# A graph kernel whose neighbour aggregation is reorganised: nodes ordered by degree, smaller sorting networks, neighbour lists from packed words

## The chip, the core and the metric

The kernel runs on one core of a Trainium2 chip. A core has a matrix engine (TensorE, in the profile PE, with its weight loads listed apart as PEld), a vector engine (VectorE, DVE), an engine for functions of one input (ScalarE, ACT), GpSimd (POOL), which here issues the gathers, and SyncE (SP), which issues the plain transfers. Each engine works through its own instructions in order; semaphores tie the engines together. The metric is device time in microseconds (us), lower is better.

## What is computed

The input is 16 graphs (B) of 1,024 nodes (N) with 64 channels (C): `x` is 16 x 1024 x 64, `adj` is 16 x 1024 x 1024 of zeros and ones, symmetric, ones on the diagonal, and every node is unmasked. An edge between two different nodes is drawn with probability 0.0078125 on each side of the diagonal and then mirrored, from a fixed seed. Two layers follow each other, each closed by a layer norm over the channels of "input plus layer output".

```python
# layer 0, cut to what matters
nb = (adj > 0) & ~eye                       # neighbours without the node itself
m = nb.sum(-1); rank = cumsum(nb) - 1
skip = where(m > 10, (m + 1) // 2, 1)
removed = nb & (skip > 1) & mask & ((rank + 1) % skip == 0)
adj_d = where(removed | removed.T, 0, adj_with_self_loops)
sv = sort(where(adj_d > 0, x[neighbour], big))          # per node and channel
agg = 0.25*q(0.25) + 0.5*q(0.5) + 0.25*q(0.75)          # interpolated quantiles of sv
x = layernorm(x + (relu((x + agg) @ W1 + b1) @ W2 + b2) * mask)
# layer 1
x = layernorm(x + (tanh(concat(x, adj @ x) @ V1 + c1) @ V2 + c2))
```

So each node drops at most two of its neighbours (and loses those that dropped it), and then, channel by channel, takes a weighted sum of three quantiles of what its remaining neighbours and itself hold.

## The kernel before, in words

Nodes lie along the 128 partitions, eight tiles (NT) of 128 nodes per graph. The 16 graphs are unrolled. A scheduler places each engine's instructions; buffers in rotating pools decide how far one graph's work may run into the next.

**Which neighbours stay.** `dilate` (L125-164) loads one row tile of `adj` after another, transposes it on TensorE into `adj_t` for layer 1, and finds on VectorE, with a prefix sum (L143) and two comparisons (L156, L157), what each row removes. `neighbours` (L166-176) transposes the removals on TensorE, combines them with what the row keeps (L173) and counts the row (`deg`).

**The list of neighbours.** For each row tile, L317 multiplies the 0/1 row by "1024 minus column", and five rounds of MAX8 (L319) and MATCH_REPLACE8 (L321) over all 1,024 columns pull out up to K = 40 neighbour numbers, the node itself among them. Empty places get a number that no row of `x` has.

**Gather, sort, weigh.** `terms(t)` (L328-339) fills a tile `g` of 40 slots x 64 channels with a large number (L330), issues 40 indirect transfers from GpSimd (L332), each of which fetches one slot's row of `x` for the 128 nodes and skips the empty ones, and sorts the 40 slots with a bitonic network on VectorE (`sort40`, L258-284; `exchange`, L243-256; L255 is the minimum and L256 the maximum of a pair). L338 multiplies the sorted slots by the quantile weights. There are three buffers for `g`.

**The rest of both layers.** `finish` (L190-240) sums the 40 weighted slots with 40 f32 matmuls against the identity (L199), runs the two small dense layers (L202, L206), a layer norm (L178-188), the message matmul against `adj_t` (L225), the second small network (L229, L233) and the second layer norm.

**The general path.** `degree` holds every node's count. At the end its maximum is read into a register (L345-352), and `tc.If(largest > K)` (L354) guards a second implementation that recomputes all nodes of all graphs without a limit on neighbours. It is a loop over the 16 graphs, and within it a loop over the 64 channels (L373). One turn of the inner loop:

- VectorE copies the channel (`x_c`), TensorE transposes it into a row along every partition with 8 matmuls, ScalarE copies that out in two halves (`x_r`);
- for each of 8 node tiles k, VectorE writes whether node k comes no later than node j, for all j: comparisons over the tiles before k and after k (L387, L389) and two instructions of 128 x 128 on the diagonal (L390, L392);
- for each of 8 row tiles and 2 halves of 512 nodes (16 units), TensorE counts with 8 bf16 matmuls of 128 x 512 how many valid neighbours come no later (`p_cnt`, two buffers); ScalarE makes of that, for each of the three quantiles, an absolute value with a bias per partition (L407) and a rectified 1 - |.| (L408), into `u` (two buffers); VectorE adds the three up with their shares, multiplies by the 0/1 row, and multiplies by `x_r` with a running sum;
- VectorE adds the two halves into `agg`.

After the 64 channels `finish` runs for that graph. In the program this code stands once; the loops repeat it.

Of the kernel before, what the change touches and what calls it, by code (L numbers as in the profile page):

```python
# [1 line left out]

# [7 lines left out]
F32 = mybir.dt.float32  # L10
F16 = mybir.dt.float16
BF16 = mybir.dt.bfloat16
# [7 lines left out]
P = 128  # L20
K = 40          # neighbours that the sorted path holds per node
BIG = 8.0e37    # sorts behind every value of a node feature; its weight is 0
OOB = 65536.0   # an index that no row of x has: the gather skips it
# [3 lines left out]
EPS = 1e-5  # L27


@with_exitstack  # L30
def kernel(
# [24 lines left out]
    rows = ctx.enter_context(tc.tile_pool(name="rows", bufs=2))  # L56
    held = ctx.enter_context(tc.tile_pool(name="held", bufs=NT))
    work = ctx.enter_context(tc.tile_pool(name="work", bufs=2))
    ps_t = ctx.enter_context(tc.tile_pool(name="ps_t", bufs=2, space=PSUM))
    ps_m = ctx.enter_context(tc.tile_pool(name="ps_m", bufs=2, space=PSUM))  # L60

# [7 lines left out]
    upper = const.tile([P, P], F32, name="upper")  # row <= column  # L69
# [3 lines left out]
    ones_row = const.tile([P, N], BF16, name="ones_row")  # L73
    nc.vector.memset(ones_row, 1.0)
    down = const.tile([P, N], F32, name="down")  # N - column
    nc.gpsimd.iota(down, pattern=[[-1, N]], base=N, channel_multiplier=0,
                   allow_small_or_imprecise_dtypes=True)
    slot = const.tile([P, K], F32, name="slot")
    nc.gpsimd.iota(slot, pattern=[[1, K]], base=0, channel_multiplier=0,
                   allow_small_or_imprecise_dtypes=True)  # L80
    big = const.tile([P, 1], F32, name="big")
    nc.vector.memset(big, BIG)
    eps = const.tile([P, 1], F32, name="eps")
    nc.vector.memset(eps, EPS)
    degree = const.tile([P, B * NT], F32, name="degree")
# [21 lines left out]
    # node mask: a node per partition, a tile of nodes per column  # L107
# [5 lines left out]
    mask_p = ps_m.tile([P, 512], F32, name="mask_p", tag="m")  # L113
    nc.tensor.transpose(mask_p[:, :B * NT], mask_f, ident[:B * NT, :B * NT])
    nc.scalar.copy(mask, mask_p[:, :B * NT])
# [4 lines left out]
    def load_x(b):  # L120
        t = work.tile([P, NT, C], F32, name="x_s")
        nc.sync.dma_start(t, x[b].rearrange("(t p) c -> p t c", p=P))
        return t

    def dilate(adj_b, mask_b):  # L125
        """The neighbours that stay by each row's own rule, those it removes, and adj transposed."""
        adj_t = work.tile([P, NT, N], F32, name="adj_t", bufs=1)
        kept, removed = [], []
        for t in range(NT):
# [12 lines left out]
            rank = rows.tile([P, N], F16, name="rank", bufs=1)  # from 1; exact up to 2048  # L142
            nc.vector.tensor_tensor_scan(rank, ones_row, nb, 0.0, op0=ALU.mult, op1=ALU.add)  # L143
            # skip = ceil(m / 2); ranks skip and 2 * skip go where m > T_THRESH and the mask is set
# [21 lines left out]
    def neighbours(t, kept, removed, deg):  # L166
        """Row tile t of the dilated adjacency, self-loops included, as 0 and 1; its row sums."""
        blk = slice(t * P, (t + 1) * P)
        p = ps_t.tile([P, N], BF16, name="p_rem", tag="tr")
        for j in range(NT):  # L170
            nc.tensor.transpose(p[:, j * P:(j + 1) * P], removed[j][:, blk], ident_h)  # L171
        v = rows.tile([P, N], BF16, name="valid")
        nc.vector.scalar_tensor_tensor(v, p, 0.5, kept[t], op0=ALU.is_lt, op1=ALU.mult, accum_out=deg)  # L173
        nc.vector.tensor_add(v[:, blk], v[:, blk], ident_h)
        nc.vector.tensor_scalar(deg, deg, 1.0, None, op0=ALU.add)
        return v

    def layer_norm(s, dst):  # L178
        st = work.tile([P, 3, NT], F32, name="ln_st")
        nc.vector.tensor_reduce(st[:, 0], s, AX.X, ALU.add)  # L180
        nc.vector.tensor_scalar(st[:, 0], st[:, 0], 1.0 / C, None, op0=ALU.mult)
        nc.vector.tensor_sub(s, s, bcast(st[:, 0], C))
        sq = work.tile([P, NT, C], F32, name="ln_sq", bufs=1)
        nc.scalar.activation(sq, s, AF.Square)
        nc.vector.tensor_reduce(st[:, 1], sq, AX.X, ALU.add)
        nc.scalar.activation(st[:, 2], st[:, 1], AF.Sqrt, bias=eps, scale=1.0 / C)
        nc.vector.reciprocal(st[:, 2], st[:, 2])
        nc.vector.tensor_mul(dst, s, bcast(st[:, 2], C))

    def finish(out_b, x_s, mask_b, adj_t, terms):  # L190
        """Both layers from the aggregates on: terms(t) are the matrices whose sum is tile t's."""
        p_y = ps_m.tile([P, NT, C], F32, name="p_y", tag="y", bufs=1)
        for h in range(2):
            g_t = work.tile([C, HALF], F32, name="g_t")
            for t in range(HT):
                p = ps_m.tile([P, 512], F32, name="p_g", tag="g", bufs=1)
                todo = terms(h * HT + t)
                for i, term in enumerate(todo):
                    nc.tensor.matmul(p[:C, :P], term, ident, start=(i == 0), stop=(i == len(todo) - 1))  # L199
                nc.scalar.copy(g_t[:, t * P:(t + 1) * P], p[:C, :P])  # L200
            p = ps_m.tile([P, 512], F32, name="p_h", tag="m")
            nc.tensor.matmul(p[:H, :HALF], w1a_s, g_t, start=True, stop=True)  # L202
            h_t = work.tile([H, HALF], F32, name="h_t")
            nc.scalar.activation(h_t, p[:H, :HALF], AF.Relu, bias=b1a_c)
            for t in range(HT):
                nc.tensor.matmul(p_y[:, h * HT + t, :], h_t[:, t * P:(t + 1) * P], w2a_s,  # L206
                                 start=True, stop=True)
        y = work.tile([P, NT, C], F32, name="y", bufs=1)
        nc.vector.tensor_add(y, p_y, b2a_r[:, None, :].to_broadcast([P, NT, C]))
        nc.vector.tensor_mul(y, y, bcast(mask_b, C))  # L210
        nc.vector.tensor_add(y, y, x_s)
        x1 = work.tile([P, NT, C], F32, name="x1", bufs=1)
        layer_norm(y, x1)

        p_d = ps_m.tile([P, NT, C], F32, name="p_d", tag="y", bufs=1)
        for h in range(2):
            cols = slice(h * HALF, (h + 1) * HALF)
            node_t = work.tile([2 * C, HALF], F32, name="node_t")
            p = ps_m.tile([P, 512], F32, name="p_x", tag="m")
            for t in range(HT):  # L220
                nc.tensor.transpose(p[:C, t * P:(t + 1) * P], x1[:, h * HT + t, :], ident)
            nc.scalar.copy(node_t[:C], p[:C, :HALF])
            p = ps_m.tile([P, 512], F32, name="p_msg", tag="m")
            for j in range(NT):
                nc.tensor.matmul(p[C:2 * C, :HALF], x1[:, j, :], adj_t[:, j, cols],  # L225
                                 start=(j == 0), stop=(j == NT - 1))
            nc.scalar.copy(node_t[C:], p[C:2 * C, :HALF])
            p = ps_m.tile([P, 512], F32, name="p_z", tag="m")
            nc.tensor.matmul(p[:C, :HALF], w1b_s, node_t, start=True, stop=True)  # L229
            z_t = work.tile([C, HALF], F32, name="z_t")  # L230
            nc.scalar.activation(z_t, p[:C, :HALF], AF.Tanh, bias=b1b_c)
            for t in range(HT):
                nc.tensor.matmul(p_d[:, h * HT + t, :], z_t[:, t * P:(t + 1) * P], w2b_s,  # L233
                                 start=True, stop=True)
        d = work.tile([P, NT, C], F32, name="d", bufs=1)
        nc.vector.tensor_add(d, p_d, b2b_r[:, None, :].to_broadcast([P, NT, C]))  # L236
        nc.vector.tensor_add(d, d, x1)
        o = work.tile([P, NT, C], F32, name="o")
        layer_norm(d, o)
        nc.sync.dma_start(out_b.rearrange("(t p) c -> p t c", p=P), o)  # L240

# [1 line left out]
    def exchange(dst, src, lo, n, k, j, up):  # L243
        """Compare-exchange over slots lo .. lo + n at distance j; blocks of k slots go upward
        and downward in turn, or all the way that `up` says."""
        s = src[:, lo:lo + n, :].rearrange("p (q k) c -> p q k c", k=k)
        d = dst[:, lo:lo + n, :].rearrange("p (q k) c -> p q k c", k=k)
        ways = ((0, 2, True), (1, 2, False)) if up is None else ((0, 1, up),)
        for first, step, asc in ways:
            if first >= n // k:  # L250
                continue
            sv = s[:, first::step].rearrange("p q (m two j) c -> p q m two (j c)", two=2, j=j)
# [194 lines left out]
```

## Time and profile before

| | |
|---|---|
| time, median of 3 runs | 12,840.29 us (12,827.75 to 12,854.84) |
| span of the profiled execution | 11,693.4 us |
| mean granted TensorE clock | 0.580 of full speed |
| VectorE | 9,848.3 us busy, 84% of the span |
| GpSimd | 6,903.3 us busy, 59% |
| TensorE | 2,196.3 us busy, 19% |
| ScalarE | 664.9 us busy, 6% |
| indirect gathers (L332) | 5,120, mean 1,348 ns |
| general path (L354-418) | no instruction of it in the trace |

The profiled execution's span runs from its first to its last instruction; no separate time is given for that execution, and the median of the timed runs lies 1,146.9 us above its span. Busy shares are averages over stages; the span is cut below by stage. A group's line reads: program line, engine, operation, output <- input, shapes, count, then busy time and mean of one, then the idle time of that engine just before and what ended it.

### The profile page before, as it was taken

Reading aid. Unit: us, or ns where it says so; the run is one execution under the profiler, and the core shown is the slowest. Engines: PE = TensorE matmul, PEld = TensorE weight load, DVE = VectorE, ACT = ScalarE, POOL = GpSimd, SP = SyncE. Lnnn points to the kernel's source line nnn. Section 1 sums busy time; section 2 is a strip of 40 time slices with the busy share of each in tenths; the row PEclk is TensorE's granted clock in tenths of the full one; section 3 lists DMA queues with packets and bytes.
Section 4 is the critical chain, followed back from the end, with each engine's and each line's share of the span. In section 5 each row is a group of like instructions: output and inputs, shape, how many; then the busy total and the mean of one; then the engine's idle time right before and its main releaser. Section 6 shows DMA issues by size and latency. Waiting matters only on the chain. (4 is left out here: it accounts for less than half of the span.)

```text
span 11693.4 us, 53638 instructions
## 1 busy us (share of the span) xinstructions
PE 2196.3 (19%) x13826; PEld 1809.5 (15%) x13826; DVE 9848.3 (84%) x12969; ACT 664.9 (6%) x835; POOL 6903.3 (59%) x5130
## 2 busy tenths in 40 slices
PE   1121111211112121121211212112121221211212
PEld 1111111111111111111111112111120111101111
DVE  8888888888888888888888888888888888888887
ACT  0000000000000000000000000000000000000000
POOL 5828558285582855828558284582846828468284
PEclk5565555655556555565555655556565555655556
DMA  1000000000000000000000000000000000000000
GB/s 30 7 19 7 5 22 7 19 7 5 22 7 19 7 4 22 7 18 7 5 22 7 18 8 5 22 7 19 8 5 22 7 20 7 5 22 7 12 7 5
DMA packets 216974, 141.12 MB, mean 12 GB/s; under 512 B 164598, under 2 KB 180495, under 8 KB 216656
## 3 DMA queue, kind: packets, MB, share of 16 engines
q0 software_dynamic: 163840, 61.91, 2.9%
q1 hardware_dynamic: 52816, 75.71, 2.1%
q8 instruction: 110, 1.80, 0.1%
q14 instruction: 208, 1.70, 0.0%
HBM read 239.27 MB, written 4.19 MB: 21 GB/s over the span
## 5 line engine op out<-in xcount | busy, mean ns | idle before, releaser
L332 POOL DMA_INDIRECT g<-in_x_dram,idx x5120 | 6901.2, 1348 | 4648.6 <-issue 4546.5
L255 DVE TENSOR_TENSOR h<-g 128x512 f32<-128x512 f32 (+4 forms) x1920 | 1754.2, 930 | 1359.3 <-DMA g<-in_x_dram,idx 1358.9
L199 PE MATMUL p_g<-ident,h 128*64 128x128 f32 x10240 | 1430.9, 312 | 7457.8 <-DVE h L338 7457.8
L199 PEld LDWEIGHTS p_g<-ident,h 128*64 128x64 f32 x10240 | 1400.0, 162 | 7487.9 <-DVE h L338 7487.9
L255 DVE TENSOR_TENSOR g<-h 128x512 f32<-128x512 f32 (+4 forms) x1920 | 1813.7, 947 | 0.2
L256 DVE TENSOR_TENSOR g<-h 128x512 f32<-128x512 f32 (+4 forms) x1920 | 1813.8, 947 | 0.0
L256 DVE TENSOR_TENSOR h<-g 128x512 f32<-128x512 f32 (+4 forms) x1920 | 1753.5, 930 | 0.0
L319 DVE MAX8 key<-code 128x8 f32<-128x1024 f32 x640 | 753.4, 1211 | 0.0
L330 ACT COPY g<-big 128x2560 f32<-128x2560 f32 x128 | 297.3, 2324 | 6679.3 <-DVE h L338 6679.3
L321 DVE MATCH_REPLACE8 code<-key,code 128x1024 f32<-128x1024 f32 x512 | 616.4, 1208 | 0.0
L171 PE MATMUL p_rem<-ident_h,removed 128*128 128x128 bf16 x1024 | 142.9, 299 | 1752.4 <-DVE removed L159 903.8
L171 PEld LDWEIGHTS <-removed 128*128 128x128 bf16 x1024 | 98.7, 134 | 1795.6 <-DVE removed L159 927.4
L338 DVE TENSOR_TENSOR h<-g,qw 128x2560 f32<-128x2560 f32 x128 | 360.2, 2814 | 0.0
L236 DVE TENSOR_TENSOR d<-p_d,b2b_r 128x512 f32<-128x512 f32 x16 | 11.1, 692 | 367.9 <-PE p_d L233 367.9
L143 DVE TENSOR_TENSOR_SCAN rank<-ones_row,nb 128x1024 f16<-128x1024 bf16 x128 | 292.3, 2283 | 0.5
L225 PE MATMUL p_msg<-adj_t,x 128*64 128x512 f32 x512 | 255.4, 657 | 0.0
L137 PE MATMUL p_adj<-ident,a 128*128 128x128 f32 x1024 | 156.8, 298 | 78.1 <-DMA a<-in_adj_dram 63.2
L296 ACT ACTIVATE hat<-hat 128x320 f32<-128x320 f32 x48 | 22.5, 470 | 2542.2 <-DVE hat L295 2542.2
L157 DVE SCALAR_TENSOR_TENSOR hit<-rank,s,hit 128x1024 bf16<-128x1024 f16 x128 | 164.1, 1282 | 3.5
L317 DVE TENSOR_TENSOR code<-valid,down 128x1024 f32<-128x1024 bf16 x128 | 154.8, 1212 | 0.0
L173 DVE SCALAR_TENSOR_TENSOR valid<-p_rem,kept 128x1024 bf16<-128x1024 bf16 x128 | 154.2, 1214 | 0.0
L138 ACT COPY adj_t<-p_adj 128x512 f32<-128x512 f32 x256 | 140.5, 586 | 70.7 <-PE p_adj L137 69.8
(88 smaller groups left out, 1797.1 us busy)
## 6 DMA issues: line engine op xcount, KB each, us to landing
g<-in_x_dram,idx POOLq DMA_INDIRECT x5120, 2.5
a<-in_adj_dram SPq DMA_DIRECT2D x128, 512.0 KB, 3.7
x_s<-in_x_dram SPq DMA_DIRECT2D x16, 256.0 KB, 2.9
out_dram<-o SPq DMA_DIRECT2D x16, 256.0 KB, 4.1
w1a_s<-in_L_gnn_W_dram SPq DMA_DIRECT2D x1, 32.0 KB, 2.0
w2a_s<-in_L_gnn_W_dram SPq DMA_DIRECT2D x1, 32.0 KB, 1.8
w1b_s<-in_L_gnn_W_dram SPq DMA_DIRECT2D x1, 32.0 KB, 1.9
b2a_r<-in_L_gnn_b_dram SPq DMA_DIRECT2D x1, 32.0 KB, 3.8
```

The lines of the kernel that those rows point to most:

```text
L143: nc.vector.tensor_tensor_scan(rank, ones_row, nb, 0.0, op0=ALU.mult, op1=ALU.add)
L157: nc.vector.scalar_tensor_tensor(hit, rank, t2, hit, op0=ALU.is_equal, op1=ALU.add)
L171: nc.tensor.transpose(p[:, j * P:(j + 1) * P], removed[j][:, blk], ident_h)
L199: nc.tensor.matmul(p[:C, :P], term, ident, start=(i == 0), stop=(i == len(todo) - 1))
L225: nc.tensor.matmul(p[C:2 * C, :HALF], x1[:, j, :], adj_t[:, j, cols], start=(j == 0), stop=(j == NT - 1))
L255: nc.vector.tensor_tensor(dv[:, :, :, low], sv[:, :, :, 0], sv[:, :, :, 1], op=ALU.min)
L256: nc.vector.tensor_tensor(dv[:, :, :, high], sv[:, :, :, 0], sv[:, :, :, 1], op=ALU.max)
L319: nc.vector.max(key[:, t, r:r + 8], code)
L321: nc.vector.match_replace(code, key[:, t, r:r + 8], code, 0.0)
L330: nc.scalar.copy(g.rearrange("p k c -> p (k c)"), big.to_broadcast([P, K * C]))
L332: nc.gpsimd.indirect_dma_start(out=g[:, k, :], out_offset=None, in_=x_rows, in_offset=bass.IndirectOffsetOnAxis(ap=idx[:, t, k:k + 1], axi ...
L338: nc.vector.tensor_mul(h, g, bcast(weights[:, t], C))
```

## The change

The unguarded path is rewritten; the general path keeps its loops, its tiles and its arithmetic.

- **Order by degree** (`find`). Removal, counting and the 0/1 rows move from VectorE scans to TensorE matmuls with ScalarE reading PSUM. From each node's neighbour count (without itself) its place in the order of falling degree is counted with matmuls, and a permutation matrix brings the nodes' data into that order.
- **Lists from words.** TensorE packs each row's 1,024 zeros and ones into 128 words: word c has bit k set where node 128k + c is a neighbour. MAX8 and MATCH_REPLACE8 pick the non-empty words. A loop of `BITS = 4` rounds takes the highest bit of every word, writes 16,256 + 128k + c, and removes that bit. A second MAX8 / MATCH_REPLACE8 pass picks the codes.
- **Slots by tile.** `CAPS = (36, 20, 18, 16, 15, 14, 12, 11)` are the slots of the eight tiles in order of degree, the node itself among them: 134 gathers a graph in place of 320, four or fewer buffers ahead.
- **Pruned networks.** `network(n)` builds, while the program is made, an odd-even merge network for n slots, keeps only the exchanges that the quantile places can depend on, and works within one tile of twice n slots; empty slots hold large numbers of either sign in turn, so that the middle stays in the middle.
- **Back** (`close`): the aggregates are split into three bf16 parts and brought back to node order by matmuls; the transposed adjacency is made from a second load of `adj`.
- **The guard.** `over` takes two numbers per partition and graph: the largest excess of a count over its tile's slots, and the count of all neighbours minus the count of all list entries. The general path runs where the largest of all of them is above 0.

```diff
-K = 40
+CAPS = (36, 20, 18, 16, 15, 14, 12, 11)
+CODE = 127 * 128
+BITS = 4
...
+        for i in range(BITS):
+            nc.vector.tensor_scalar(top, rest.bitcast(I32), 0x7F800000, None, op0=ALU.bitwise_and)
+            nc.vector.tensor_scalar(high, top, 16, None, op0=ALU.logical_shift_right)
+            nc.vector.tensor_add(codes[:, i], high, where)
+            if i + 1 < BITS:
+                nc.vector.tensor_sub(rest, rest, top.bitcast(F32))
...
+        nc.vector.tensor_sub(short, degree, caps)
+        nc.vector.tensor_reduce(over[:, 2 * b:2 * b + 1], short, AX.X, ALU.max)
+        nc.vector.tensor_reduce(sums[:, 0:1], degree, AX.X, ALU.add)
+        nc.vector.tensor_scalar(listed, code, float(CODE), None, op0=ALU.is_ge, op1=ALU.add,
+                                accum_out=sums[:, 1:2])
+        nc.vector.tensor_sub(over[:, 2 * b + 1:2 * b + 2], sums[:, 0:1], sums[:, 1:2])
...
+        for k in range(1, n):
+            nc.gpsimd.indirect_dma_start(out=g[:, k, :], ...)
+        steps, ends = network(n)
+        for op, box in steps:
+            nc.vector.tensor_tensor(cells(g, box, 2, C), cells(g, box, 0, C), cells(g, box, 1, C), op=op)
...
+        found = find(0, ps, rows, mats, lists)
+        for b in range(B):
+            x_s, x_q, number, index, weights = found
+            if b + 1 < B:
+                found = find(b + 1, ps, rows, mats, lists)
+            for q in range(NT):
+                aggregate_tile(q, x_q, index, weights, agg, ps, sorts)
+            close(b, x_s, number, agg, ps, rows, mats, lists)
...
-    nc.vector.tensor_reduce(most, degree, AX.X, ALU.max)
+    nc.vector.tensor_reduce(most, over, AX.X, ALU.max)
...
-    with ... tc.If(largest > K), tc.For_i(0, B, 1) as b:
+    with ... tc.If(largest > 0), tc.For_i(0, B, 1) as b:
         x_s = load_x(b)
...
         with tc.For_i(0, C, 1) as c:
```

## The prediction, made before the changed kernel ran

> **What bounds the kernel now.** I read the page's engine sums first, then one graph cut by stage, then the waits.
>
> ```profile
> PE 2196.3 (19%) x13826; PEld 1809.5 (15%) x13826; DVE 9848.3 (84%) x12969; ACT 664.9 (6%) x835; POOL 6903.3 (59%) x5130
> ```
>
> VectorE has the most work, but no engine is full. The windows of the second graph say why (columns: stretch, its length, busy time and instructions of PE, PEld, DVE, ACT and POOL, then granted clock, DMA share, GB/s):
>
> ```profile
> 700.00:830.00 130.00, 48.80 (x246) 29.51 (x247) 100.85 (x173) 20.93 (x32) 0.00 (x0) 0.67 0.12 36
> 830.00:1427.00 597.00, 84.10 (x618) 78.80 (x617) 510.22 (x634) 21.58 (x21) 433.35 (x320) 0.56 0.04 7
> ```
>
> For 130 us neighbours are found and GpSimd has nothing; for 597 us VectorE sorts and GpSimd gathers.
>
> ```profile
> POOL g L332 <- issue: 4546.5, 5105, 200.7
> DVE h L255 <- DMA g<-in_x_dram,idx: 1358.9, 96, 26.8
> DVE d L236 <- PE p_d L233: 367.9, 16, 25.2
> ```
>
> The sort waits 1,359 us for gathers in all. VectorE bounds the kernel, GpSimd close behind. No instruction of L354-418 is in the trace: the largest count was at most 40.
>
> **The guard, before any price.** What the change costs hangs on one comparison, so I worked it out from the reference's seeded input. That the chip had this input the trace shows: the gathers' packet bytes, added up by graph, differ between neighbouring graphs by exactly 252 bytes for each list entry by which my lists differ (first two graphs 3,843,360 and 3,848,400 bytes, 14,520 and 14,540 entries). Every ordered tile fits: at most 32, 18, 16, 14, 13, 12, 10, 9 neighbours against 35, 19, 17, 15, 14, 13, 11, 10 slots. But the packed words do not. A word holds the eight columns that agree modulo 128, and four bits are taken from it. Of 2,097,152 words two hold four neighbours and one holds five: node 825 of graph 13 keeps 20, 148, 404, 788 and 916, all 20 modulo 128. Node 20 is the lowest bit and stays unlisted; that partition's counts exceed its list by 1, `over` is 1, and `largest > 0` holds. With five rounds no word would be left over. So the changed kernel runs the new path and then the general path: 16 x 64 = 1,024 turns of a loop that before never ran.
>
> **The new path, added up per graph.** Sorting: 289 instructions a graph with 79,744 elements per partition, for 62 a tile, 496 a graph, before. The rows 512 in 680 ns, 1,024 in 1,215 and 1,280 in 1,481 lie on 148 + 1.042 n ns, so 42.8 + 83.1 = 126 us; before, L255, L256, L276, L277 and L338 gave 59.9 us a tile, 479 a graph. Weighing: 16 instructions, 5,376 elements, 8 us. Thirty-two passes over 1,024 elements (eight at 0.695 like L140, the others f16 or bf16 like L156 at 0.482): 17 us. Lists: 42 MAX8 and 26 MATCH_REPLACE8 over some 100 to 160 elements; by the slope of L319 and L321 about 0.3 each, 21 us. About 20 bit operations on 168 elements, 6; eight PSUM sums, 3; `finish` as before, 9; some 40 small ones, 12. VectorE: 202 us. GpSimd: 134 gathers at 1.348 + 0.30 between them, 221 us. TensorE gets about 240 matmuls of 300 to 512 columns (0.43 each for f32 at full clock, L225) and 370 small ones (0.14 to 0.21), 103 + 65 us, beside the others' work; ScalarE about 70. Finding for the next graph is placed among this graph's sorts, so its matmul chains are covered; GpSimd ends last: 16 x 221 = 3,536, plus the first graph's finding (about 160) and the last one's end (about 60), plus 7% for waits: **4,000 us** against 11,693. Bounds: 3,300 (all VectorE) and 5,300 (the two never overlap beyond half).
>
> **One turn of the channel loop.** No row shows it, but its parts have rows of the same shape or near it, from the groups kept apart by form, and a window at the trace's end that is dense in f32 matmuls of 512 columns:
>
> ```profile
> L140 DVE TENSOR_SCALAR nb<-a 128x1024 bf16<-128x1024 f32 x128 | 88.9, 695 | 14.4 <-DMA a<-in_adj_dram 14.4
> L204 ACT ACTIVATE h_t<-p_h,b1a_c 128x512 f32<-128x512 f32 x32 | 22.0, 687 | 38.8 <-PE p_h L202 38.8
> L301 DVE SCALAR_TENSOR_TENSOR qw<-hat,qw 128x320 f32<-128x320 f32 x32 | 15.5, 484 | 0.0
> L184 ACT ACTIVATE ln_sq<-d 128x512 f32<-128x512 f32 x16 | 10.1, 633 | 4.4 <-DVE d L182 4.4
> ```
>
> ```profile
> 11662.00:11667.30 5.30, 5.28 (x13) 1.48 (x11) 0.00 (x0) 0.00 (x0) 0.00 (x0) 1.00 0.00 0
> ```
>
> - Start: x_c 0.2 (L181, eight elements), eight transposes at 0.21 (L137, 24 in 5.09 us), the second copy 0.59 (L138): 2.5 us.
> - Order matrix: 14 comparisons, 7,168 elements; L140 (1,024 in 0.695) gives 0.15 + 0.53 n, so 5.9; 16 of 128 x 128 at 0.22 to 0.28 (L174; the line above), 3.9: 9.8 us. Counting can't end before it.
> - 16 units. ScalarE: three times 0.687 (L204: from PSUM with a bias) and 0.631 (L184): 3.95 us. VectorE, one scaling, two scale-and-adds (L301's 484 ns for 320 elements lies on the sort's line, 0.686 for 512), one product and one product with a sum: 0.42 + 2 x 0.686 + 0.68 + 0.77 = 3.24. TensorE: eight matmuls of 512 columns; L225 as f32 takes 0.43 each at clock 1.00 (the window) and 0.86 in the 3 us before it at 0.53, so eight take at most 3.4 at full clock; bf16 can hardly be dearer. ScalarE sets the pace, with one catch: with two buffers for `u` its first instruction of a unit waits until VectorE has used the second; following both orders by hand with 0.04 us a handover (PE to ACT: 11649.23 to 11649.28) adds about 0.25. **4.2 us** a unit, 67.2, and 0.4 for the first count.
> - Tail: VectorE's last three and the sum, 2.3 us.
> - Edge: all engines meet and branch back. The nearest rows are the program's start, where ACT and DVE wait 0.82 and 1.10 us for the others, and a transfer's landing, 2.0 to 3.7: from 1 to 8 us. I take 4.
>
> Sum 86.2 us; times 1,024, **88,300 us**. The Trainium skill (Runtime: NRT & Kernel Launch, Instruction fetch mechanics) speaks against a loop here: a taken branch outside the fetched window must fetch its target first. No run here shows a taken branch; the 4 us leave room for it.
>
> Outside the channel loop, per graph: removal as in `dilate` 7.7 us a tile, the rows 2.1 a tile, 78 with its start 88; `finish` 40 as at the end of the trace (11,648 to 11,688); edges and transfers 12: 140 us, 2,200 in all.
>
> **Sum.** 4,000 + 88,300 + 2,200 = 94,500 us of span. Around the span: the median stands 1,147 above it, and nothing tells whether that is a constant or a share (1.098). I take the constant: 95,600. The skill's page (same, preamble/postamble breakdown) puts the launch at about 15 us; by it the sum would be 94,515, but this case's 1,147 disagrees.
>
> **Rivals.**
> 1. *The guard stays shut.* If one link of my count is wrong (a word's fifth bit counted elsewhere, or `over` not set), only the new path runs: 4,000 + 1,147 = **5,150 us**, 0.4 times the time before. For it: the slots fit every tile with one to spare. Against: the arithmetic is exact in integers, and one missed entry of 217,572 suffices. It decides from `over` = 0. 7.5%.
> 2. *TensorE paces the units.* If bf16 matmuls cost what f32 do at half clock, eight take 6.9 us and so does a unit: 86.2 + 16 x 2.7 = 129 a turn, with the rest **140,000 us**. The mean clock of 0.58 speaks for it; against it that the clock rises to 1.00 in dense stretches (L225 at 11,662) and that these would be dense. 6%.
> 3. *ScalarE and VectorE take turns* because of the two `u` buffers: 3.95 + 3.24 = 7.2 a unit, **145,000**. Against: VectorE's share for one buffer (0.42 to 0.69) fits under the next ScalarE instruction. 4%.
>
> **Range.** Low: 3.95 a unit, edge 1, order matrix 8.5: 77 a turn, 79,000 + 5,100 + 0 = 84,000. High: 4.6 a unit (handovers of 0.2), edge 8: 98 a turn, 100,000 + 7,500, and the share around it in part: 113,000. My case has 82%, nearly all of it within this range; the rivals lie outside. Measurement can tell some 0.2% from no change. Slower by more: 92% (mine, 2 and 3); faster by more: 7.5% (rival 1); within it: the half per cent left, for no case gives it.
>
> **What would show it.** Right: the busy tenths show GpSimd at work in the first 4% of the span and then no more; ABS and RELU of 128x512 x49,152 each on ScalarE, the largest group; p_cnt x131,072 on TensorE; turns of 86 us; gathers x2,144. Wrong in a size: a different turn, and then the idle before the first ABS of a unit (handover), before x_c (edge) or before p_cnt (order matrix). Wrong altogether: no p_cnt, a span near 4,000.

## The result and the profile after

| | before | after |
|---|---|---|
| time, median | 12,847.24 us (4 runs, 12,827.75 to 12,854.84) | 85,945.64 us (4 runs, 85,938.51 to 85,950.26) |
| ratio | | 6.691, 95% interval 6.682 to 6.700 |
| profiled execution: time, span | span 11,693.4 us | 85,946.24 us, 85,944.5 us |
| granted TensorE clock | 0.580 | 0.767 |

The kernel is slower by the mechanism that was forecast: the guard opens, and the general path runs behind the new one (the experiments below show it). First the engine sums and two rows of the busy tenths of the changed kernel:

```profile
PE 45634.2 (53%) x157186; PEld 18121.9 (21%) x157186; DVE 64843.4 (75%) x142256; ACT 60619.6 (71%) x102595; POOL 2418.3 (3%) x2163
...
ACT  2257777777777777777777777777777777777777
POOL 4510000000000000000000000000000000000000
```

Each digit is the busy share of a slice of 2,149 us, in tenths. GpSimd works in the first two slices and a little of the third, and then no more; from there on every slice looks like the next. That is a loop. Its groups (busy time, mean ns of one, idle time before it and what ended it):

```profile
L736 PE MATMUL p_cnt<-before,val_t 128*128 128x512 bf16 x131072 | 40379.4, 455 | 25522.1 <-ACT u L742 22387.4 <-DVE before L724 1429.3 <-DVE before L722 995.2
L742 ACT ACTIVATE u<-p_cnt,shift 128x512 f32<-128x512 f32 x49152 | 32210.0, 681 | 13497.2 <-PE p_cnt L736 9191.7 <-DVE w L747 4297.1
L743 ACT ACTIVATE u<-u 128x512 f32<-128x512 f32 x49152 | 28990.4, 623 | 526.4
L747 DVE SCALAR_TENSOR_TENSOR w<-u,w 128x512 f32<-128x512 f32 x32768 | 22676.1, 692 | 12545.8 <-ACT u L743 10833.7
```

The counts are those of 16 x 64 turns with 16 units of three quantiles each: 49,152 and 131,072. TensorE waits most for ScalarE, VectorE waits for ScalarE, and ScalarE waits 9,192 us for the first count of a turn and 4,297 us for VectorE. The timeline of ScalarE shows one unit from one ABS to the same one of the next unit:

```profile
40002.41 0.69 ACT L742 ACTIVATE u<-p_cnt,shift 128x512 f32<-128x512 f32 x1 [0.30 <-DVE w L747]
40003.13 0.63 ACT L743 ACTIVATE u<-u 128x512 f32<-128x512 f32 x1
40003.66 1.27 ACT L742 ACTIVATE u<-p_cnt,shift 128x512 f32<-128x512 f32 x2
40004.84 1.14 ACT L743 ACTIVATE u<-u 128x512 f32<-128x512 f32 x2
40006.28 0.69 ACT L742 ACTIVATE u<-p_cnt,shift 128x512 f32<-128x512 f32 x1 [0.30 <-DVE w L747]
```

A unit takes 3.87 us, of which 0.30 is a wait for a `u` buffer that VectorE still reads. Two more rows of the timeline mark the edge between two turns and the first unit of a turn:

```profile
40040.82 0.17 DVE L710 COPY x_c<-x_s 128x8 f32 x1 [1.24 <-PEq L708]
...
40052.67 1.27 ACT L742 ACTIVATE u<-p_cnt,shift 128x512 f32<-128x512 f32 x2 [9.04 <-PE p_cnt L736]
```

The turn's start `x_c` (L710) stands at 9,622.1, 9,699.2 and 9,776.3 us in one graph. In the mean of all turns it is 77.04 us a turn, 78,890 us for 1,024. The new path ends at about 4,830 us; some 2,225 us are left for what lies outside the channel loop, 139 a graph.

### The profile page after: what moved, and what is told of

The parts are those of the page before. It is cut to its first block, busy times and chain, and to the rows that moved or that the text cites. A ratio compares the mean times of both kernels' runs of the same rounds, so it can differ in the third digit from the quotient of the medians.

```text
span 85944.5 us, 674929 instructions
## 1 busy us (share of the span) xinstructions
PE 45634.2 (53%) x157186; PEld 18121.9 (21%) x157186; DVE 64843.4 (75%) x142256; ACT 60619.6 (71%) x102595; POOL 2418.3 (3%) x2163
## 5 line engine op out<-in xcount | busy, mean ns | idle before, releaser
L736 PE MATMUL p_cnt<-before,val_t 128*128 128x512 bf16 x131072 | 40379.4, 455 | 25522.1 <-ACT u L742 22387.4
L742 ACT ACTIVATE u<-p_cnt,shift 128x512 f32<-128x512 f32 x49152 | 32210.0, 681 | 13497.2 <-PE p_cnt L736 9191.7
L747 DVE SCALAR_TENSOR_TENSOR w<-u,w 128x512 f32<-128x512 f32 x32768 | 22676.1, 692 | 12545.8 <-ACT u L743 10833.7
L743 ACT ACTIVATE u<-u 128x512 f32<-128x512 f32 x49152 | 28990.4, 623 | 526.4
L736 PEld LDWEIGHTS <-val_t 128*128 128x128 bf16 x131072 | 14437.0, 110 | 51278.9 <-issue 42370.1
L748 DVE TENSOR_TENSOR w<-w,val 128x512 f32<-128x512 f32 x16384 | 11326.9, 691 | 558.0
L749 DVE SCALAR_TENSOR_TENSOR w<-w,x_r 128x512 f32<-128x512 f32 x16384 | 11224.9, 685 | 34.8
L745 DVE TENSOR_SCALAR w<-u 128x512 f32<-128x512 f32 x16384 | 6996.9, 427 | 1560.5 <-ACT u L743 1560.5
L725 DVE SCALAR_TENSOR_TENSOR before<-x_r,x_c,upper 128x128 bf16<-128x128 f32 x8192 | 2833.6, 346 | 1870.2 <-ACT x_r L716 1870.2
L722 DVE TENSOR_SCALAR before<-x_r,x_c 128x128 bf16<-128x128 f32 (+6 forms) x7168 | 3441.1, 480 | 0.0
L724 DVE TENSOR_SCALAR before<-x_r,x_c 128x896 bf16<-128x896 f32 (+6 forms) x7168 | 3361.5, 481 | 43.4
L727 DVE SCALAR_TENSOR_TENSOR before<-x_r,x_c,before 128x128 bf16<-128x128 f32 x8192 | 2834.2, 346 | 36.0
L563 PE MATMUL p_agg<-h,ident 128*128 128x64 f32 x2688 | 519.5, 369 | 1308.2 <-DVE h L560 864.6
L710 DVE COPY x_c<-x_s 128x8 f32 x1024 | 175.8, 172 | 1254.0 <-PEq L708 1250.6
L541 ACT COPY g<-fill 128x2240 f32<-128x2240 f32 (+7 forms) x128 | 138.6, 1085 | 1144.0 <-DVE h L560 639.9
L563 PEld LDWEIGHTS p_agg<-h,ident 128*128 128x128 f32 x2688 | 502.6, 283 | 1329.4 <-issue 1276.3
```

Source lines behind the costliest of these rows:

```text
L722: nc.vector.tensor_scalar(before[:, k, :k], x_r[:, :k], x_k, None, op0=ALU.is_gt)
L724: nc.vector.tensor_scalar(before[:, k, k + 1:], x_r[:, k + 1:], x_k, None, op0=ALU.is_ge)
L725: nc.vector.scalar_tensor_tensor(before[:, k, k], x_r[:, k], x_k, upper, op0=ALU.is_equal, op1=ALU.mult)
L727: nc.vector.scalar_tensor_tensor(before[:, k, k], x_r[:, k], x_k, before[:, k, k], op0=ALU.is_gt, op1=ALU.add)
L736: nc.tensor.matmul(p[:, :HALF], val_t[:, k, t * P:(t + 1) * P], before[:, k, js].rearrange("p q j -> p (q j)"), start=(k == 0), stop=(k == ...
L742: nc.scalar.activation(u, p[:, :HALF], AF.Abs, bias=shift[:, i, t:t + 1])
```

## Experiments

A time without a range is that of a single run.

### Is it the guard, and by how much does it open?

`bits5` takes a fifth bit out of each packed word; `over1` keeps four and lets one unlisted neighbour pass, so it leaves out one neighbour of one node.

```diff
-BITS = 4
+BITS = 5
```
```diff
-        tc.If(largest > 0),
+        tc.If(largest > 1),
```

> The changed kernel with a fifth round in the loop that takes bits from the words, and nothing else. Theory (one unlisted neighbour opens the guard): every neighbour is listed, the guard stays shut, and only the new path runs: 4,830 us in the changed kernel's trace, plus 16 times about 5 us for the fifth round and the wider second pass over the codes, so 4,850 to 4,950 us, 0.38 times the time before. Rival (the guard opens for another reason: a tile whose slots are too few, or a count that never comes out even): the general path runs again and the time stays near 85,950 us.

> The changed kernel with four rounds as it is, and the guard at 'above 1' in place of 'above 0'; it leaves out one neighbour of one node. Theory: the largest excess is exactly 1 (one neighbour of node 825 in graph 13), so the guard is shut: 4,820 to 4,850 us. Rival (several unlisted neighbours on one partition, or a tile that lacks more than one slot): the excess is 2 or more and the time stays near 85,950 us.

Measured: `bits5` 4,911.7 us (4,910.2 to 4,914.7), 0.3817 of the kernel before, interval 0.3811 to 0.3823; `over1` 4,855.8 us, 6 above its range. With a guard at 1 the general path stays shut, with a guard at 0 it runs: the largest excess is exactly 1. With a fifth bit it stays shut at 0 as well: the excess comes from the words. Which word it is the runs don't show; the seeded input has one with five bits, that of node 825 in graph 13. It costs 85,946 - 4,856 = 81,090 us. A fifth round of bit operations with the wider second pass over the codes, some 56 us by these two times, takes it away.

### Does the cost belong to the general path, which the change didn't touch?

`before_forced` is the kernel before with its guard opened (`largest > 1` in place of `largest > K`), so that it runs both paths.

> The kernel before with its guard at 'above 1' in place of 'above 40', so that its own general path runs as well. Theory (the cost is that of the general path, whichever kernel it stands in): 12,847 + 1,024 turns of 77.1 us + 16 times 137 us = 93,960 us, to within 300. Rival (the changed kernel made the general path dearer, by its pools or by what runs beside it): clearly below that, under 92,000 us.

Measured 94,272.4 us. Its own path ends at 12,846, which leaves some 81,400 for the general one against 81,090 in the changed kernel. The groups of the untouched code there answer to those above:

```profile
L407 ACT ACTIVATE u<-p_cnt,shift 128x512 f32<-128x512 f32 x49152 | 32295.6, 681 | 13519.2 <-PE p_cnt L401 9201.5 <-DVE w L412 4307.9
L408 ACT ACTIVATE u<-u 128x512 f32<-128x512 f32 x49152 | 28989.3, 623 | 526.2
```

The sum came out 312 us above what was expected, 12 more than the margin given: a turn takes 77.24 us in the mean there against 77.04, and the work outside the channel loop 145 us a graph against 139. The general path is thus no dearer in the changed kernel (the rival), but 0.4% cheaper: the slowdown is the old fallback, entered.

### What paces a unit of the loop?

`u4` gives `u` four buffers instead of two.

```diff
-                        u = dense.tile([P, HALF], F32, name="u", bufs=2)
+                        u = dense.tile([P, HALF], F32, name="u", bufs=4)
```

> The changed kernel, general path included, with four buffers for u in place of two. Theory (each unit of the channel loop loses 0.30 us while ScalarE waits for VectorE to release a buffer of u): a unit takes 3.57 in place of 3.87 us, 16,384 units, so 4,900 us less: 81,050 us. Rival (VectorE or the two count buffers hold the unit, and the wait only moves there): within 800 us of 85,945.

Measured 77,261.9 us, 8,684 less than the changed kernel and 3,788 less than expected; the turn is 68.5 us. ScalarE's groups there, one of VectorE's, and a piece of ScalarE's timeline:

```profile
L742 ACT ACTIVATE u<-p_cnt,shift 128x512 f32<-128x512 f32 x49152 | 34460.0, 827 | 9161.8 <-PE p_cnt L736 9161.2
L743 ACT ACTIVATE u<-u 128x512 f32<-128x512 f32 x49152 | 31888.1, 778 | 0.0
L747 DVE SCALAR_TENSOR_TENSOR w<-u,w 128x512 f32<-128x512 f32 x32768 | 22628.6, 691 | 4285.9 <-ACT u L743 2566.0
```
```profile
40001.01 1.37 ACT L742 ACTIVATE u<-p_cnt,shift 128x512 f32<-128x512 f32 x2
40002.15 1.26 ACT L743 ACTIVATE u<-u 128x512 f32<-128x512 f32 x2
40003.19 1.38 ACT L742 ACTIVATE u<-p_cnt,shift 128x512 f32<-128x512 f32 x2
```

The wait for VectorE is gone, as the theory has it. But the gain is 0.53 us a unit (8,684 us over 16,384 units) and not 0.30: with four buffers the schedule also puts the next ABS ahead of the RELU that must wait for its own ABS (0.72 us between the two starts above, where others are 0.53 to 0.59 apart). ScalarE still sets the pace: two ABS and two RELU come every 2.18 us, three of each every 3.27, and within the units it waits for nothing; L742's idle time is that for the first count. VectorE waits for ScalarE (2,566 us at L747), but it has little left to spare: its six instructions of a unit last 0.42 + 4 x 0.69 + 0.08 = 3.26 us end to end. The idle time in the row was less than what the change gained, because the change altered the order of the instructions too.

### Where were the 1,147 us between the span and the median before?

> The kernel before, unchanged, profiled once more. Theory: the 1,147 us that I put around the span lie inside it, in an execution that was slower than the profiled one all along; the span is then 1.7 us below the time, about 12,860, and the graphs follow each other some 800 us apart where it was 731. Rival: something of 1,147 us stands around the span; the span is then about 11,700 with a time of 12,850.

`before_look` took 12,875.9 us with a span of 12,874.2. So 1.7 us stand around the span; the first profiled execution was itself shorter. VectorE's waits in the new one (in all, times, longest), to be read beside the two rows that the prediction shows of the old:

```profile
DVE h L255 <- DMA g<-in_x_dram,idx: 1559.7, 80, 47.8
DVE d L236 <- PE p_d L233: 365.5, 16, 25.1
DVE key L319 <- remote: 198.7, 100, 4.0
DVE hat L295 <- remote: 81.8, 23, 3.7
```

"remote" is a wait that ended on a semaphore's update for which the trace finds no sender near that time. The senders are there, but earlier, as the trace's semaphore records show beside the ends of the instructions that raise them. Call an update late when the next record of its semaphore comes over 0.3 us after its instruction's end. In the first profile of before, no update of TensorE, VectorE or ScalarE is late. In `before_look` 1,224 are, 1,206 of them while GpSimd gathers. In the changed kernel it is 1,428, 1,417 of them while GpSimd gathers, and not one after its last gather at 4,755.7 us, though the general path raises some 240,000. Several instructions can share one late record (`before_look` has 7,239 records for 7,801 raising instructions of VectorE, the first profile 7,803), so these counts are rough; the idle time is not. VectorE's waits that end on "remote" add up to 550 us in `before_look`, against 0 in the first profile, of the 1,181 us between the two spans. The gathers themselves are slower too: 5,120 in 7,340.9 us busy against 6,901.2.

The runs met several chips. Where before took 12,828 to 12,877 us the profiles show late updates; where it took 11,674 to 11,702 (`fill_pool` and the runs with it, below) they show three at most. No chip is known to have been met twice, so a property of the chip and one of the time are not told apart.

### What holds the new path?

GpSimd gathers for 2,465 of `bits5`'s 4,908 us. Its waits there:

```profile
POOL g L544 <- ACT g L541: 1025.2, 14, 75.9
POOL g L544 <- issue: 635.3, 2082, 1.4
POOL g L544 <- DVE listed L508: 297.2, 14, 22.3
POOL g L544 <- ACT g L542: 287.4, 17, 89.5
```

L541 and L542 are ScalarE's copies into a free buffer `g`. I took the number of buffers for the cause. The kernels of this group ran where updates come late. All three kernels of this group have five bits. `g2` has two for the tiles below the top one instead of three, `g4` four of fitted sizes; `unpruned` leaves the buffers and makes the networks larger.

```diff
-                       bufs=1 if q == 0 else 3)
+                       bufs=1 if q == 0 else 2)              # g2
```
```diff
-        g = sorts.tile([P, 2 * n, C], F32, name="g", tag="g_top" if q == 0 else "g",
-                       bufs=1 if q == 0 else 3)
+        g = sorts.tile([P, 2 * n, C], F32, name="g", tag="g_top" if q == 0 else f"g{(q - 1) % 4}",
+                       bufs=1)                               # g4; `listed` goes into codes[:, 0]
```
```diff
-    live, kept = set(needed(n)), []
+    live, kept = set(range(n)), []                           # unpruned
```

> Five bits, and two buffers for the sorted tiles below the top one where there were three. Theory: how far GpSimd may gather ahead is set by these buffers, so one fewer costs about one tile's gathers in each graph, 14 to 19 at 1.3 us, 16 times 18 to 25: 5,200 us (5,100 to 5,350). Rival: GpSimd's own gathers and the finding of the neighbours set the period of a graph, then 4,910 within 30.

> Five bits, and four buffers of fitted sizes for tiles 1 to 7 (tiles 1 and 5, 2 and 6, 3 and 7 share one, tile 4 has its own) where three were shared. Theory: the buffers hold GpSimd (it waits 1,025 + 287 us for their fill copies), so one more is worth some 14 to 16 gathers at 1.3 us in each graph, 250 to 300 us: 4,640 us (4,550 to 4,750). Rival: the order of ScalarE's queue holds the fill copies, not the buffers: 4,900 within 30.

> Five bits, and networks in which every comparison keeps both of its outputs: 320 instructions and 86,144 elements per partition in a graph against 289 and 79,744, 11.3 us more of VectorE a graph by 148 + 1.042 n ns, 180 us in all. Theory: VectorE and GpSimd hand the buffers to each other, so part of it is on the path: 60 to 180 us more, 4,970 to 5,090. Rival: GpSimd alone sets the end: within 20 us of 4,910.

Measured: `g2` 4,783.1, `g4` 5,164.1, `unpruned` 4,999.2 us. The theory of the buffers falls: one fewer is 129 us faster, one more 252 slower, both against its sign, and the rivals of `g2` and `g4` (no change beyond 30 us) fall as well. In `unpruned` VectorE works 180.3 us more, as worked out, and the time grows by 88, within the range given; its rival, GpSimd alone, falls. That these 88 us are VectorE's work is not shown, though: `g2` and `g4` moved the time by more with VectorE's work within 30 us of `bits5`'s. What goes wrong in `g4` can be seen at one place of its timeline (lines of TensorE, ScalarE and VectorE):

```profile
2335.78 3.09 PE L563 MATMUL p_agg<-h,ident 128*128 128x64 f32 x14
...
2357.06 1.54 PE L591 MATMUL p_adj<-ident,a 128*128 128x128 f32 x6 [17.55 <-ACT adj_t L592]
```

```profile
2409.29 0.21 ACT L564 COPY agg<-p_agg 128x64 f32<-128x64 f32 x1 [51.24 <-remote]
```

```profile
2410.18 0.69 DVE L573 TENSOR_TENSOR left<-agg,parts 128x512 f32<-128x512 f32 x1 [47.66 <-issue]
```

L564 copies out what TensorE summed at L563. It waits for TensorE's semaphore alone; the sum had ended at 2,338.87, all of TensorE's work by 2,358.6, and the update arrives at 2,409.26. The busy time of the engines between (window, its length, PE, PEld, DVE, ACT, POOL, clock, DMA share, GB/s):

```profile
2358.70:2409.20 50.50, 0.00 (x0) 0.00 (x0) 2.69 (x3) 0.00 (x0) 38.85 (x38) 0.50 0.10 24
```

For 50 us GpSimd issues 38 gathers one behind the other and next to nothing else happens on the core; VectorE stands at L573, with the next graph's sort behind it in its queue. That wait (VectorE's L573 for L572) sums to 90 us in `g2`, 288 in `bits5` and 640 in `g4`. That longer stretches of gathers make it worse is argued from these three and not shown: the schedule of every engine differs between them too, and the number of late updates (1,544, 1,527, 1,071) does not grow. Nor does this wait alone set the time: in `unpruned` it is 67 us, and that kernel is slower than `bits5`.

### Pauses between gathers, other copies, no gathers

All three kernels again have five bits. `fill_pool` moves both copies into the buffer (L541, L542) from ScalarE to GpSimd; `fill_each` fills each slot by a short GpSimd instruction beside its gather; `nogather` has no gathers.

```diff
-        nc.scalar.copy(g[:, 1:n], fill[:, 1:n, None].to_broadcast([P, n - 1, C]))
-        nc.scalar.copy(g[:, 0], x_q[:, q])
+        nc.gpsimd.tensor_copy(g[:, 1:n], fill[:, 1:n, None].to_broadcast([P, n - 1, C]))
+        nc.gpsimd.tensor_copy(g[:, 0], x_q[:, q])            # fill_pool
```
```diff
-        nc.scalar.copy(g[:, 1:n], fill[:, 1:n, None].to_broadcast([P, n - 1, C]))
...
         for k in range(1, n):
+            nc.gpsimd.memset(g[:, k], -BIG if k % 2 else BIG)   # fill_each
             nc.gpsimd.indirect_dma_start(
```

> Five bits, and the copies that fill a buffer ahead of its gathers (fill and the node's own row) on GpSimd in place of ScalarE, in bulk as before. Theory: what holds GpSimd is that semaphores of the other engines arrive late while it gathers, not ScalarE's queue; GpSimd gets eight copies more a graph, so 4,880 to 5,100 us. Rival: the fill copies' place in ScalarE's queue holds GpSimd (it waits 1,025 + 287 us for them): 4,300 to 4,600.

> Five bits, and the fill of each slot as a short GpSimd instruction of 64 elements beside the gather into it (the schedule puts mostly three of them, then three gathers) in place of ScalarE's bulk copy. Theory: semaphores of the other engines arrive late (1,527 of them by over 0.3 us in the five-bit kernel, by up to 99 us) because gathers follow each other with only 0.30 us between; pauses let them through: fewer than 1,000 late ones and 4,450 to 4,800 us, though GpSimd works some 500 us more. Rival: they are late beside gathers at any spacing: 4,900 to 5,400.

> Five bits, the gathers left out and the fill zero, so that the neighbours' rows are not read (the aggregate is then that of zeros and the node itself). Theory: with no gathers no semaphore arrives late and no buffer is waited for; VectorE's 2,650 us of work and the chains of a graph's end set the time: 3,000 to 3,500 us, with no wait that nothing in the trace explains. Rival: the late semaphores come from something else: over 3,900 us and those waits still there.

Measured 4,130.1, 4,132.9 and 3,051.8 us, but on a chip on which the kernel before took 11,679.9 us, and with 3, 2 and 0 late updates. So the three do not tell the theories apart: the late updates were missing whether gathers were paced, moved or left as dense as before. `fill_pool` and `fill_each` came out below every range given for them, theory's and rival's. The three runs show two things. With next to no late updates a new path of nearly the same work takes 4,130, and without gathers, in `nogather`, it takes 3,052 with VectorE at 86%. And gathers alone don't make updates late: `fill_pool` issues 2,144 of them, and on that chip three updates are late. `fill_pool_timed` is `fill_pool` once more, for a comparison with `bits5` where updates come late.

> The kernel with five bits and the fill copies on GpSimd once more, timed against the kernel before. The first look at it met a chip on which the kernel before took 11,680 us and no semaphore arrived late, where it had been 12,866 to 12,876 with late ones for the five-bit kernel. If the kernel before takes 11,680 again: 4,130 us, ratio 0.3536. If it takes 12,870: by the theory that late semaphores and not the fill copies cost the five-bit kernel its 4,912, it is 4,850 to 5,100 (ratio about 0.385); by the rival that the copies held GpSimd, 4,250 to 4,600.

It met updates in time again: 4,134.6 us (4,131.6 to 4,137.2) against 11,689.4 (11,673.7 to 11,702.5), ratio 0.3536, interval 0.3530 to 0.3542. VectorE's longest waits in `fill_pool` have no row without a sender any more; the last line is GpSimd's longest wait for another engine:

```profile
DVE g L551 <- DMA g<-in_x_dram,index: 833.0, 60, 41.8
DVE d L315 <- PE p_d L312: 239.1, 16, 24.9
DVE g L551 <- POOL g L542: 77.3, 4, 20.5
DVE g L551 <- POOL g L541: 74.5, 4, 19.3
...
POOL g L541 <- DVE h L560: 600.3, 30, 27.1
```

L560 is VectorE's weighing of the sorted slots, the last to read a buffer `g`. So where updates come in time, GpSimd does wait for a buffer, 600 us in all. What one buffer more or fewer does there was not tried: the theory of the buffers fell only where updates come late.

`fill_pool` and `fill_each` are the fastest versions that gather, and `bits5` and `fill_pool` both beat the kernel before and the changed one. How much of 0.3817 to 0.3536 is the copies' move and how much the chip (or the time) stays open: `bits5` was not run where updates come in time, nor `fill_pool` where they come late.

## Why the prediction was right, and which terms were mis-sized

- **The guard.** Right, and by the count given: `over1` and the changed kernel together show an excess of exactly 1. This step decided between 5,150 and 95,600; the profile of before alone could not have told it.
- **One turn, 86.2 us.** Measured 77.04. Units: 16 x (4.2 - 3.87) = 5.3 us of the 9.2. I added ScalarE's rows end to end (3.95), but in a row of independent ones the next starts before the last has ended: two ABS take 1.27 us and two RELU 1.14, and the six with their starts 0.53 to 0.72 apart take 3.57. The wait for `u`, put at 0.25, is 0.30. Edge: 4 us, measured 1.24 (idle before `x_c`), another 2.8. Start, order matrix and first count: 12.7, measured 11.85 (40,040.82 to 40,052.67); the diagonal comparisons are dearer than thought (L725 and L727 0.34 to 0.35 against 0.22 to 0.28), but most of the 0.59 us copy of the second half is hidden. Tail 2.3, measured 2.1.
- **The loop edge and the page.** The prediction cited the Trainium skill (Runtime: NRT & Kernel Launch, Instruction fetch mechanics) against a loop. The trace's 1.24 us a turn holds whatever such a fetch costs, together with all engines' meeting: 1,270 us of 85,946.
- **TensorE paces the units (rival 2).** No: 40,379 us over 16,384 units is 2.5 us a unit, where the rival had 6.9. **ScalarE and VectorE in turn (rival 3).** No: 3.87 and not 7.2; `u4` shows that four buffers in place of two are worth 0.53, a wait of 0.30 and a better order of ScalarE's instructions.
- **Outside the channel loop.** 140 a graph, measured 139.
- **The new path, 4,000 us.** In the changed kernel 4,830, mis-sized by a fifth. The work was if anything overrated: VectorE 2,611 us in 4,771 (163 a graph against 202), GpSimd 2,418 and 0.30 between gathers (191 against 221). The allowance of 7% for waits is what failed: handovers that the profile of before showed in time come late here, and GpSimd waits 1,048 and 274 us for ScalarE's fill copies L541 and L542. Whether late updates hold these copies or their place in ScalarE's queue was not told apart. Where updates came in time, `fill_pool` took 4,130; the changed kernel was not run there.
- **Around the span, 1,147 us.** Wrong: 1.7 us (85,946.24 less 85,944.5). The difference lay between two executions of before, inside their spans.

Together: 95,600 less 9,410 (turns), less 1,145 (around), plus 830 (new path), plus 25 (outside the channel loop) is 85,900; measured 85,946. The result lies near the low end of the range. The 84,000 has 77 us a turn, which is what was measured, so the result stands above it only by the rest: some 7,055 us where the low end has 5,100. And that end was added wrongly. With 3.95 a unit, an edge of 1 and an order matrix of 8.5 the parts of a turn come to 77.9 us and not 77, and 5,100 is less than the low bound of the new path and the work outside the loop, 3,300 + 2,200. Added rightly the low end is 85,270, and the result is above it by 676 us: without the new path's excess of 830 us it would lie below, so such a range would have held by luck. "ABS and RELU the largest group" was wrong in the order (TensorE's p_cnt is larger by its busy time), and GpSimd ends at 5.5% of the span rather than 4%.

## What to carry to other kernels

Where a change comes with a fallback behind a test on the data, work out the test on the actual data before any price: one item out of 217,572 decided between a ratio of 0.38 and one of 6.7. In a chain of engines with few buffers, read a unit's length from start to start of the same instruction; sums of durations overstate an engine with overlapping instructions, and the idle time shown need not be what more buffers give (0.30 us shown, 0.53 gained), since they change the order of instructions too. Before a span is compared with a median, profile the same kernel on the chip that gave the times.

## What the runs showed of the hardware that was not expected

- In some groups of runs semaphore updates of TensorE, ScalarE and VectorE arrive late while GpSimd issues gathers, by up to 29.8, 112.4 and 81.0 us for VectorE, ScalarE and TensorE in the changed kernel; in the others, with the same kind of gathers, three at most do. The kernel before took 12,876 us in the former and 11,680 in the latter. Why they differ, how much of these 10% the late updates make, and whether pauses would help where updates come late, was not settled.
- ScalarE's instructions on 512 elements overlap: 0.69 us for one from PSUM, 1.27 for two in a row.
- At the edge of this loop, whose turn has about 500 instructions, VectorE stands idle for 1.24 us.
